# Four-head graph attention: its preparation by pairs of tiles in a fixed TensorE order, with the first scores as columns of the projection

## The chip, the cores and the metric

The kernel runs on one core of one Trainium2 chip. The metric is the time of one execution on the device in microseconds (us), as the median of several runs. A core has TensorE (PE: matmuls and, on rows of their own, the loads of the stationary operand, PEld), VectorE (DVE), ScalarE (ACT), GpSimd (POOL) and SyncE (SP, which issues DMAs here). Each takes its instructions in order from its own queue and waits on semaphores for the others. Matmul results land in PSUM, from where VectorE or ScalarE brings them to SBUF.

## The reference, cut to what matters

The network has four layers on a graph of N = 2708 nodes with 256 features. Each layer is a graph attention and a feed-forward part, and both add to `x`. The change is in the graph attention of the second layer (layer 1 in the code), which has H = 4 heads of D = 64:

```python
x = _layernorm(x)                               # (2708, 256)
h  = (x @ W).reshape(n, H, D)
si = jnp.einsum('nhd,d->nh', h, a1)             # first scores, one per node and head
sj = jnp.einsum('nhd,d->nh', h, a2)             # second scores
e  = leaky_relu(si[:, None, :] + sj[None, :, :], negative_slope=0.2)
e  = where(adj[:, :, None] > 0, e, -9e15)
att = softmax(e, axis=1)
out = einsum('ijh,jhd->ihd', att, h)            # added to x
```

The kernel never forms `e` by itself. With slope 0.2, exp(leaky_relu(si + sj)) is exp(0.2 si) exp(0.2 sj) max(1, exp(0.8 si) exp(0.8 sj)). The factor exp(0.2 si) falls out of the softmax over j. So three tables are wanted: exp(0.8 si) for all i, spread over all 128 partitions (`big_p`, one row of 2708 columns per head, the same on every partition); exp(0.8 sj) as one number per node on its partition (`ratio`); and exp(0.2 sj), which multiplies the projected features (`V`) and makes the denominators (`low`).

## The kernel before

The nodes are cut into NT = 22 tiles of up to 128 (`tiles`, the last has 20), and the columns into six chunks of up to 512 (`cols = chunks(512)`: five of four tiles, and one of 148 columns with two tiles). `X[:, t, :]` holds tile t with nodes on partitions.

Right before, `slice_ffn` ends with 22 tiles of four matmuls each (tile `po`, L477 through the helper's L139), added to `X` by VectorE (L478). The layer-norm statistics (`net.ln_stats()`, L773) follow each `X` tile closely: `bn_stats` and `bn_aggr` on VectorE (L160, L161), then for each four tiles a square root on ScalarE (L163) and a reciprocal on VectorE (L167).

`gat_heads` (L704) then prepares the tables (L756 to L819) and runs the attention (L820 to L882). Before the loop of the preparation it folds `a1` and `a2` into the weight `W` (`fold_scores`, L768 and L769), so that the second scores are four more columns of the projection weight `w`, and the first scores have a weight of their own, `spread`, whose columns 0, 32, 64 and 96 hold the four heads and the rest zeros. Then, for each chunk of columns:

- for each tile of the chunk: VectorE normalizes it into `f` (L780, helper L124); TensorE transposes its two halves into PSUM `tp` (L781, helper L132); ScalarE copies them into the chunk's `ft` (L782); TensorE projects, 260 columns, into `pv` (L784, helper L139); ScalarE takes two exponentials of the four score columns, into `low` (L787) and `ratio` (L788); VectorE multiplies the features into `V` (L789);
- for the chunk: VectorE sums `ft` (L795); TensorE multiplies `spread` with `ft` into `s1p` (L797), so that each head's first scores stand as a row on partition 0, 32, 64 or 96; ScalarE copies it to `s1` (L799); one-row matmuls with ones (L803) spread each head's row over all partitions into `pp`, four banks of PSUM; ScalarE takes the exponential of all four heads into `big_p` (L804).

A PSUM tile named `tp`, `s1p` or `pp` has one buffer, `pv` two. A matmul of these float32 tiles appears as two records, a transpose as one. After the loop come the mean row for nodes without neighbours (L806 to L815) and the transposed flags of such nodes (L817, L818), sent into the mask by `mark_empty`.

The order of the preparation is the Tile framework's: it arranges each engine's queue by the program's order and by its own estimate of when operands are ready. A pool's memory goes to the next pool when its tiles are released; the attention's `e` tiles (L820) take the place of the preparation's `g1one` and `g1work`. In the attention itself TensorE's order is written out (`tc.manual_schedule`, L826): for each of two pairs of heads and each tile j, ScalarE computes max(1, .) less 1 (L700), VectorE adds one and applies the mask (L701), and TensorE accumulates values (L836) and denominators (L847).

Of the kernel before, what the change touches and what calls it, by code (L numbers as in the profile page):

```python
# [48 lines left out]
def tiles_of(start, length):  # L49
    return range(start // P, (start + length + P - 1) // P)  # L50
# [653 lines left out]
def gat_heads(net, keep):  # L704
# [38 lines left out]
    with ExitStack() as ctx:  # L743
        big = ctx.enter_context(tc.tile_pool(name="g1big", bufs=1))
        big_p = big.tile([P, H, N], F32, name="big_p")
        ratio = big.tile([P, NT, H], F32, name="ratio")
        V = big.tile([P, NT, H, DH], F32, name="V")

        low = big.tile([P, NT, H, 2 * Q - 1], F32, name="low")
# [6 lines left out]
        with ExitStack() as c1:  # L756
            one = c1.enter_context(tc.tile_pool(name="g1one", bufs=1))
            work = c1.enter_context(tc.tile_pool(name="g1work", bufs=3))
            psum = c1.enter_context(tc.tile_pool(name="g1p", bufs=1, space=PSUM))
            fsum = one.tile([P, 2], F32, name="fsum")  # L760
            spread = one.tile([P, 2, P], F32, name="spread")

            w = one.tile([P, 2, H * DH + H], F32, name="w")
            nc.gpsimd.dma_start(w[:, :, : H * DH], a["g1_w"].rearrange("(c p) m -> p c m", p=P))
            av = one.tile([P, 2, DH], F32, name="av")
            for n in range(2):
                nc.gpsimd.dma_start(av[:, n, :], a[f"g1_a{n + 1}"].partition_broadcast(P))
            a1 = fold_scores(net, one, w, av[:, 0, :].unsqueeze(1).to_broadcast([P, H, DH]), H, DH, "a1")  # L768
            a2 = fold_scores(net, one, w, av[:, 1, :].unsqueeze(1).to_broadcast([P, H, DH]), H, DH, "a2")  # L769
            nc.vector.tensor_copy(w[:, :, H * DH :], a2)  # L770
            nc.vector.memset(spread, 0.0)
            nc.vector.tensor_copy(spread.rearrange("p c (h k) -> p c h k", h=H)[:, :, :, 0], a1)
            ln = net.ln_stats()  # L773
            parts = one.tile([P, len(cols), 2], F32, name="parts")
            for n, (n0, nw) in enumerate(cols):
                ft = work.tile([P, 2, 512], F32, name="ft")
                for k, t in enumerate(tiles_of(n0, nw)):
                    r = rows(t)
                    f = work.tile([P, D], F32, name="f")
                    net.normed(f, t, ln)  # L780
                    ps = net.transposed(psum, f, r)  # L781
                    nc.scalar.copy(ft[:, :, k * P : k * P + r], ps[:, :, :r])  # L782
                    pv = psum.tile([P, H * DH + H], F32, name="pv", bufs=2)
                    net.matmul_k(pv[:r], ft[:, :, k * P : k * P + r], w)  # L784
                    s2 = pv[:r, H * DH :]
                    lt = low[:r, t, :, Q - 1]
                    nc.scalar.activation(lt, s2, AF.Exp, scale=SLOPE)  # L787
                    nc.scalar.activation(ratio[:r, t, :], s2, AF.Exp, scale=1.0 - SLOPE)  # L788
                    nc.vector.tensor_tensor(  # L789
                        V[:r, t],  # L790
                        pv[:r, : H * DH].rearrange("p (h d) -> p h d", d=DH),
                        lt.unsqueeze(2).to_broadcast([r, H, DH]),
                        ALU.mult,
                    )
                nc.vector.tensor_reduce(parts[:, n, :], ft[:, :, :nw], AX.X, ALU.add)  # L795
                ps = psum.tile([P, 512], F32, name="s1p")
                net.matmul_k(ps[:, :nw], spread, ft[:, :, :nw])  # L797
                s1 = work.tile([P, 512], F32, name="s1")
                nc.scalar.copy(s1[:, :nw], ps[:, :nw])  # L799
                ps = psum.tile([P, H, 512], F32, name="pp")  # L800
                for h in range(H):
                    row = slice(32 * h, 32 * h + 1)
                    nc.tensor.matmul(ps[:, h, :nw], net.ones[row, :], s1[row, :nw], start=True, stop=True)  # L803
                nc.scalar.activation(big_p[:, :, n0 : n0 + nw], ps[:, :, :nw], AF.Exp, scale=1.0 - SLOPE)  # L804

            nc.vector.tensor_reduce(fsum, parts.rearrange("p n c -> p c n"), AX.X, ALU.add)  # L806
            ps = psum.tile([P, H * DH + H], F32, name="pv", bufs=2)
            one_row = slice(SPARE, SPARE + 1)
            for c in range(2):
                nc.tensor.matmul(  # L810
                    ps[one_row, : H * DH], fsum[:, c : c + 1], w[:, c, : H * DH], start=c == 0, stop=c == 1
                )
            nc.vector.tensor_scalar(
                V[one_row, LAST].rearrange("p h d -> p (h d)"), ps[one_row, : H * DH], 1.0 / N, None, ALU.mult
            )  # L815
            ps = psum.tile([NT, P], F32, name="s1p")
            nc.tensor.transpose(ps, net.empty, net.ident)  # L817
            nc.vector.tensor_copy(net.flags, ps)  # L818
            mark_empty(net)  # L819
# [1630 lines left out]
```

## Time and profile before

| | |
|---|---|
| median of 3 runs | 2646.69 us (2646.11 to 2649.6) |
| the profiled execution | 2647.78 us, span 2646.0 us |
| TensorE busy over the span | 92%, mean granted clock 0.962 |
| VectorE, ScalarE, GpSimd busy | 56%, 40%, 12% |
| the preparation, first `tp` transpose to first L700 | 603.26 to 670.29 us |
| the attention that follows | 670 to about 1000 us, PE busy in all of each 20 us from 680 on |
| projections `pv` of the preparation | 84 records of 128x260 and 4 of the last tile, mean 463 ns and 386 ns |
| exponentials to `big_p` (L804) | 5 of 128x2048, 1877 ns each, one of 128x592, 663 ns |
| granted clock, 603.2 to 618.0 us | 0.65 |

The span runs from the first instruction to the last. Times inside the kernel are counted from the span's start. A row of the profile names a line of the code, an engine, an operation, its output and its inputs; a line can be a helper's, so that the projections of several stages share L139 and are told apart by tile. A matmul's record includes its way through the pipeline, so back-to-back matmuls start closer together than their durations.

### The profile page before, as it was taken

Reading aid. Unit: us, or ns where it says so; the run is one execution under the profiler, and the core shown is the slowest. Engines: PE = TensorE matmul, PEld = TensorE weight load, DVE = VectorE, ACT = ScalarE, POOL = GpSimd, SP = SyncE. Lnnn points to the kernel's source line nnn. Section 1 sums busy time; section 2 is a strip of 40 time slices with the busy share of each in tenths; the row PEclk is TensorE's granted clock in tenths of the full one; section 3 lists DMA queues with packets and bytes.
Section 4 is the critical chain, followed back from the end, with each engine's and each line's share of the span. In section 5 each row is a group of like instructions: output and inputs, shape, how many; then the busy total and the mean of one; then the engine's idle time right before and its main releaser. Section 6 shows DMA issues by size and latency. Waiting matters only on the chain. (4 is left out here: it accounts for less than half of the span.)

```text
span 2646.0 us, 32568 instructions
## 1 busy us (share of the span) xinstructions
PE 2446.7 (92%) x11676; PEld 1581.2 (60%) x11676; DVE 1476.4 (56%) x3258; ACT 1060.2 (40%) x1714; POOL 329.2 (12%) x445
## 2 busy tenths in 40 slices
PE   5999999887999998979799989999899999969998
PEld 4666765574333334468578854444357777747887
DVE  7754348544788886333545457787653222264556
ACT  3444443313787772321434323334422222234454
POOL 1000002100000001134130011222231111110002
PEclk9999999978999999989899999999989999989999
DMA  8899520000000002774310010000231111050001
GB/s 289 281 299 320 172 86 31 3 6 1 1 1 1 1 1 82 170 193 144 91 62 1 1 38 9 19 17 17 101 128 50 33 33 33 22 203 7 1 1 43
DMA packets 106875, 197.70 MB, mean 75 GB/s; under 512 B 8846, under 2 KB 63736, under 8 KB 103876
## 3 DMA queue, kind: packets, MB, share of 16 engines
q1 hardware_dynamic: 88010, 146.82, 17.8%
q0 software_dynamic: 14896, 43.89, 5.1%
q10 hardware_dynamic: 3806, 4.85, 0.6%
q8 instruction: 98, 1.61, 0.3%
q14 instruction: 65, 0.53, 0.1%
HBM read 135.82 MB, written 59.71 MB: 74 GB/s over the span
## 5 line engine op out<-in xcount | busy, mean ns | idle before, releaser
L701 DVE SCALAR_TENSOR_TENSOR e<-e,mask 128x768 f32<-128x768 f32 (+3 forms) x352 | 417.0, 1215 | 241.9 <-ACT e L700 239.1
L700 ACT ACTIVATE e<-big_p,minus_one,ratio 128x768 f32<-128x768 f32 (+3 forms) x352 | 418.6, 1226 | 285.2 <-PE acc L1371 196.8
L1371 PE MATMUL acc<-V,e 128*128 128x257 f32 x1848 | 405.3, 382 | 5.7 <-DVE e L701 5.6
L1371 PEld LDWEIGHTS acc<-V,e 128*128 128x128 f32 x1848 | 352.7, 191 | 58.6 <-issue 7.0
L2125 PE MATMUL h<-w,ft 128*128 (+1 forms) x752 | 233.9, 452 | 1.3 <-DVE yl L1955 1.3
L307 PE MATMUL acc<-F,e 128*128 128x257 f32 (+1 forms) x924 | 212.5, 383 | 3.7 <-DVE e L303 3.4
L836 PE MATMUL acc<-e,V 128*64 128x512 f32 (+1 forms) x1056 | 209.1, 548 | 2.2 <-DVE e L701 2.2
L307 PEld LDWEIGHTS acc<-F,e 128*128 128x128 f32 (+1 forms) x924 | 171.6, 189 | 56.6 <-DVE e L303 29.2
L2142 DVE TENSOR_TENSOR hh<-hh,h 128x682 f32<-128x682 f32 x47 | 40.7, 865 | 243.7 <-PE h L2125 243.7
L2125 PEld LDWEIGHTS h<-w,ft 128*128 128x128 f32 x752 | 135.8, 191 | 57.2 <-issue 1.8
L836 PEld LDWEIGHTS acc<-e,V 128*64 128x64 f32 x1056 | 73.7, 138 | 151.3 <-issue 146.1
L1922 ACT ACTIVATE e<-sc 128x1024 f32<-128x1024 f32 (+4 forms) x131 | 107.1, 863 | 139.2 <-PE sc L1913 116.6
L303 DVE TENSOR_TENSOR e<-e,mask 128x512 f32<-128x512 f32 (+2 forms) x132 | 80.5, 621 | 141.3 <-ACT e L296 139.6
L1944 DVE TENSOR_TENSOR sum<-sum,e 128x1024 f32<-128x1024 f32 (+4 forms) x131 | 135.2, 1032 | 40.1 <-ACT e L1922 19.6
L296 ACT ACTIVATE e<-score 128x512 f32<-128x512 f32 (+2 forms) x132 | 69.4, 544 | 170.4 <-PE score L294 145.1
L2157 PE MATMUL po<-w,ht 114*128 (+1 forms) x564 | 131.5, 383 | 0.9 <-DVE ht L2150 0.9
L1913 PE MATMUL sc<-qt,kt 64*128 64x512 f32 (+5 forms) x568 | 123.9, 555 | 1.4 <-ACT sum L1922 0.9
L2157 PEld LDWEIGHTS po<-w,ht 114*128 114x128 f32 x564 | 107.6, 192 | 23.0 <-DVE ht L2150 8.2
L847 PE MATMUL den<-e,low 128*3 128x512 f32 (+1 forms) x1056 | 117.7, 542 | 0.0
L294 PE MATMUL score<-QK 128*128 128x512 f32 (+2 forms) x264 | 112.0, 553 | 3.4 <-ACT e L296 3.0
L1938 PE MATMUL po<-e,V 128*64 128x512 f32 (+5 forms) x524 | 111.2, 543 | 1.7 <-DVE e L1928 1.7
L2151 ACT COPY ht<-pt 114x256 f32<-114x256 f32 x47 | 17.5, 372 | 201.0 <-DVE ht L2150 201.0
(652 smaller groups left out, 3408.4 us busy)
## 6 DMA issues: line engine op xcount, KB each, us to landing
row<-in_adj SPq DMA_DIRECT2D x21, 1354.0 KB
raw<-in_adjT SPq DMA_DIRECT2D x35, 768.0 KB
hs<-zero SPq DMA_DIRECT2D x8, 2838.0 KB
hidden<-hr SPq DMA_DIRECT2D x32, 256.0 KB
wd<-in_f_wd SPq DMA_DIRECT2D x8, 1024.0 KB
kept<-mask SPq DMA_DIRECT2D x21, 338.5 KB
mask<-kept SPq DMA_DIRECT2D x21, 338.5 KB
w<-in_d_w1T SPq DMA_DIRECT2D x8, 682.0 KB
```

The costliest lines, as they stand in the source:

```text
L294: nc.tensor.matmul(ps[:r, :iw], QK[:, 0, span(j)], QK[:, 1, i0 : i0 + iw], start=True, stop=True)
L307: ended = nc.tensor.matmul(acc[k], e[:r, k * P : (k + 1) * P], F[:r, j, :], start=j == 0, stop=j == NT - 1)
L700: nc.scalar.activation(v, big_p[:, i], AF.Relu, bias=net.minus_one, scale=ratio)
L701: return nc.vector.scalar_tensor_tensor(v, v, 1.0, net.mask[:, j, i], ALU.add, ALU.mult)
L836: nc.tensor.matmul(acc[n][half, :iw], V[:, j, h, :], e[n][:, k, :iw], start=j == 0, stop=j == NT - 1)
L847: nc.tensor.matmul(den[g : g + Q, :iw], low[:, j, h, Q - 1 - q : 2 * Q - 1 - q], e[n][:, k, :iw], start=False, stop=j == NT - 1 and q == Q ...
L1371: nc.tensor.matmul(acc[k][:ri], e[:, k * P : k * P + ri], V[:, j, :], start=j == 0, stop=j == NT - 1)
L1913: nc.tensor.matmul(by_pairs(ps[:r, g], m, iw)[:, :, o:], kt[b, span(j)], qt[b, :, o:iw], start=True, stop=True)
L1938: nc.tensor.matmul(by_pairs(outs[n, p][b], m, iw)[:, :, o:], V[:r, j, g, :], by_pairs(e[:r, g], m, iw)[:, :, o:], start=j == 0, stop=j == ...
L1944: nc.vector.tensor_tensor(total, total, by_heads(e[:r], m, iw)[:, :, :, o:], ALU.add)
L2125: last = nc.tensor.matmul(halves[s, n][:, q, :HALF], fts[s][:, c, :], weights.w13[n][:, es[s], c, q * HALF : (q + 1) * HALF], start=c == 0 ...
L2157: last = nc.tensor.matmul(po, ht[:KP, k, :], w2[:KP, es[s], k, :], start=k == 0, stop=k == KC - 1)
```

## The change

Only the preparation in `gat_heads` is edited, and the tables' formats stay except for `ratio`.

- The folded first-score weights become columns H*DH + H to H*DH + 2H of `w`, and the second-score ones are written straight into `w`: the projection has 264 columns, and each tile's `pv` holds both scores with nodes on partitions. `s1p` and the old `spread` go.
- One exponential with scale 0.8 takes all eight score columns into `ratio`, which is now `[P, NT, 2 * H]`. GpSimd copies its four first-score columns into every 32nd column of one of four `spread` tiles, and TensorE transposes that into PSUM `line`: rows 0, 32, 64 and 96 then hold exp(0.8 si).
- VectorE copies the `line` of a chunk to `s1`; the one-row matmuls spread it over the partitions for two heads at a time (`pp` with two banks); ScalarE copies (no exponential) to `big_p`.
- Transposes go by pairs of tiles (11 pairs): four into one `tp` of two buffers, and one copy of up to 512 elements. TensorE's order is written out: the projection of a pair, the transposes of the pair two ahead, half a chunk of `pp`, the `spread` transposes of the pair before.
- The statistics of tiles 0 to 19 take the root on ScalarE as before; those of tiles 20 and 21 take three Newton steps on VectorE (`Stats.newton`, L169). An exponential of one column, queued behind the last root, loads ScalarE's table.
- `f` has four buffers, `ft` two, `pv` three.

The diff:

```diff
@@ -743,7 +743,7 @@
     with ExitStack() as ctx:
         big = ctx.enter_context(tc.tile_pool(name="g1big", bufs=1))
         big_p = big.tile([P, H, N], F32, name="big_p")
-        ratio = big.tile([P, NT, H], F32, name="ratio")
+        ratio = big.tile([P, NT, 2 * H], F32, name="ratio")
         V = big.tile([P, NT, H, DH], F32, name="V")
 
         low = big.tile([P, NT, H, 2 * Q - 1], F32, name="low")
@@ -758,53 +758,114 @@
             work = c1.enter_context(tc.tile_pool(name="g1work", bufs=3))
             psum = c1.enter_context(tc.tile_pool(name="g1p", bufs=1, space=PSUM))
             fsum = one.tile([P, 2], F32, name="fsum")
-            spread = one.tile([P, 2, P], F32, name="spread")
-
-            w = one.tile([P, 2, H * DH + H], F32, name="w")
-            nc.gpsimd.dma_start(w[:, :, : H * DH], a["g1_w"].rearrange("(c p) m -> p c m", p=P))
+            HD = H * DH
+            w = one.tile([P, 2, HD + 2 * H], F32, name="w")
+            nc.gpsimd.dma_start(w[:, :, :HD], a["g1_w"].rearrange("(c p) m -> p c m", p=P))
             av = one.tile([P, 2, DH], F32, name="av")
             for n in range(2):
                 nc.gpsimd.dma_start(av[:, n, :], a[f"g1_a{n + 1}"].partition_broadcast(P))
-            a1 = fold_scores(net, one, w, av[:, 0, :].unsqueeze(1).to_broadcast([P, H, DH]), H, DH, "a1")
-            a2 = fold_scores(net, one, w, av[:, 1, :].unsqueeze(1).to_broadcast([P, H, DH]), H, DH, "a2")
-            nc.vector.tensor_copy(w[:, :, H * DH :], a2)
-            nc.vector.memset(spread, 0.0)
-            nc.vector.tensor_copy(spread.rearrange("p c (h k) -> p c h k", h=H)[:, :, :, 0], a1)
-            ln = net.ln_stats()
+            for n in range(2):
+                fold_scores(
+                    net, one, w, av[:, n, :].unsqueeze(1).to_broadcast([P, H, DH]), H, DH, f"a{n + 1}",
+                    w[:, :, HD + (1 - n) * H : HD + (2 - n) * H],
+                )
+            spread = [one.tile([P, H, 32], F32, name=f"spread{k}") for k in range(4)]
+            for t in spread:
+                nc.gpsimd.memset(t, 0.0)
+            ln = Stats(net)
+            for t0 in range(0, NT - 2, 4):
+                ln.sums(t0, t0 + 4)
+                ln.roots(t0, t0 + 4)
+            with tc.issue_after(ln.root.ins):
+                nc.scalar.activation(one.tile([P, 1], F32, name="warm"), net.ln_eps, AF.Exp)
+            ln.sums(NT - 2, NT, root=False)
+            ln.newton(one, NT - 2, NT)
             parts = one.tile([P, len(cols), 2], F32, name="parts")
-            for n, (n0, nw) in enumerate(cols):
-                ft = work.tile([P, 2, 512], F32, name="ft")
-                for k, t in enumerate(tiles_of(n0, nw)):
+            steps = [(n, k) for n, (n0, nw) in enumerate(cols) for k in range(0, len(tiles_of(n0, nw)), 2)]
+            fts, lines = {}, {}
+
+            def pair_of(n, k):
+                return list(enumerate(tiles_of(*cols[n])))[k : k + 2]
+
+            def turn(n, k):
+                if k == 0:
+                    fts[n] = work.tile([P, 2, 512], F32, name="ft", bufs=2)
+                pair = pair_of(n, k)
+                ps = psum.tile([P, 2, 2 * P], F32, name="tp", bufs=2)
+                for m, t in pair:
+                    r, o = rows(t), (m - k) * P
+                    f = work.tile([P, D], F32, name="f", bufs=4)
+                    net.normed(f, t, (ln.mean, ln.rstd))
+                    for c in range(2):
+                        nc.tensor.transpose(ps[:, c, o : o + r], f[:r, c * P : (c + 1) * P], net.ident[:r, :r])
+                pw = (len(pair) - 1) * P + rows(pair[-1][1])
+                nc.scalar.copy(fts[n][:, :, k * P : k * P + pw], ps[:, :, :pw])
+
+            def project(n, k):
+                n0, nw = cols[n]
+                for m, t in pair_of(n, k):
                     r = rows(t)
-                    f = work.tile([P, D], F32, name="f")
-                    net.normed(f, t, ln)
-                    ps = net.transposed(psum, f, r)
-                    nc.scalar.copy(ft[:, :, k * P : k * P + r], ps[:, :, :r])
-                    pv = psum.tile([P, H * DH + H], F32, name="pv", bufs=2)
-                    net.matmul_k(pv[:r], ft[:, :, k * P : k * P + r], w)
-                    s2 = pv[:r, H * DH :]
+                    pv = psum.tile([P, HD + 2 * H], F32, name="pv", bufs=3)
+                    net.matmul_k(pv[:r], fts[n][:, :, m * P : m * P + r], w)
                     lt = low[:r, t, :, Q - 1]
-                    nc.scalar.activation(lt, s2, AF.Exp, scale=SLOPE)
-                    nc.scalar.activation(ratio[:r, t, :], s2, AF.Exp, scale=1.0 - SLOPE)
+                    nc.scalar.activation(ratio[:r, t, :], pv[:r, HD:], AF.Exp, scale=1.0 - SLOPE)
+                    nc.scalar.activation(lt, pv[:r, HD : HD + H], AF.Exp, scale=SLOPE)
+                    nc.gpsimd.tensor_copy(spread[t % 4][:r, :, 0], ratio[:r, t, H:])
                     nc.vector.tensor_tensor(
                         V[:r, t],
-                        pv[:r, : H * DH].rearrange("p (h d) -> p h d", d=DH),
+                        pv[:r, :HD].rearrange("p (h d) -> p h d", d=DH),
                         lt.unsqueeze(2).to_broadcast([r, H, DH]),
                         ALU.mult,
                     )
-                nc.vector.tensor_reduce(parts[:, n, :], ft[:, :, :nw], AX.X, ALU.add)
-                ps = psum.tile([P, 512], F32, name="s1p")
-                net.matmul_k(ps[:, :nw], spread, ft[:, :, :nw])
-                s1 = work.tile([P, 512], F32, name="s1")
-                nc.scalar.copy(s1[:, :nw], ps[:, :nw])
-                ps = psum.tile([P, H, 512], F32, name="pp")
-                for h in range(H):
-                    row = slice(32 * h, 32 * h + 1)
-                    nc.tensor.matmul(ps[:, h, :nw], net.ones[row, :], s1[row, :nw], start=True, stop=True)
-                nc.scalar.activation(big_p[:, :, n0 : n0 + nw], ps[:, :, :nw], AF.Exp, scale=1.0 - SLOPE)
+                if m * P + P >= nw:
+                    nc.vector.tensor_reduce(parts[:, n, :], fts[n][:, :, :nw], AX.X, ALU.add)
+
+            def line(n, k):
+                if k == 0:
+                    lines[n] = psum.tile([P, 512], F32, name="line")
+                for m, t in pair_of(n, k):
+                    r = rows(t)
+                    nc.tensor.transpose(
+                        lines[n][:, m * P : m * P + r],
+                        spread[t % 4][:r].rearrange("p h k -> p (h k)"),
+                        net.ident[:r, :r],
+                    )
+
+            def broadcast(n):
+                n0, nw = cols[n]
+                s1 = work.tile([P, 512], F32, name="s1", bufs=2)
+                nc.vector.tensor_copy(s1[:, :nw], lines.pop(n)[:, :nw])
+                for h0 in range(0, H, 2):
+                    yield
+                    ps = psum.tile([P, 2, 512], F32, name="pp")
+                    for m in range(2):
+                        row = slice(32 * (h0 + m), 32 * (h0 + m) + 1)
+                        nc.tensor.matmul(ps[:, m, :nw], net.ones[row, :], s1[row, :nw], start=True, stop=True)
+                    nc.scalar.copy(big_p[:, h0 : h0 + 2, n0 : n0 + nw], ps[:, :, :nw])
+
+            with tc.manual_schedule(engines={mybir.EngineType.PE}):
+                for s in range(2):
+                    turn(*steps[s])
+                later = iter(())
+                for s in range(len(steps) + 1):
+                    if s < len(steps):
+                        project(*steps[s])
+                    if s + 2 < len(steps):
+                        turn(*steps[s + 2])
+                    next(later, None)
+                    if s:
+                        line(*steps[s - 1])
+                        n, k = steps[s - 1]
+                        if s == len(steps) or steps[s][0] > n:
+                            for _ in later:
+                                pass
+                            later = broadcast(n)
+                            next(later)
+                for _ in later:
+                    pass
 
             nc.vector.tensor_reduce(fsum, parts.rearrange("p n c -> p c n"), AX.X, ALU.add)
-            ps = psum.tile([P, H * DH + H], F32, name="pv", bufs=2)
+            ps = psum.tile([P, HD + 2 * H], F32, name="pv", bufs=3)
             one_row = slice(SPARE, SPARE + 1)
             for c in range(2):
                 nc.tensor.matmul(
@@ -813,7 +874,7 @@
             nc.vector.tensor_scalar(
                 V[one_row, LAST].rearrange("p h d -> p (h d)"), ps[one_row, : H * DH], 1.0 / N, None, ALU.mult
             )
-            ps = psum.tile([NT, P], F32, name="s1p")
+            ps = psum.tile([P, 512], F32, name="line")[:NT, :P]
             nc.tensor.transpose(ps, net.empty, net.ident)
             nc.vector.tensor_copy(net.flags, ps)
             mark_empty(net)
```

## The prediction

> **What bounds the kernel now.** I read the page first. TensorE is busy 92% of the span, but that mean hides the stage that is edited, and the page's chain of waits that ended last covers only the last tiles of the kernel. So I looked up the edited lines and found that they run once, from the first `tp` transpose of this preparation at 603.26 us to the first attention activation (L700) at 670.29 us: 67.0 us of 2646.0. Then I asked for the busy time by stretches (columns: stretch, length, busy time and count of PE, PEld, DVE, ACT, POOL, then clock, DMA share, GB/s).
>
> ```profile
> 562.00:603.00 41.00, 40.25 (x177) 33.72 (x176) 25.80 (x81) 2.13 (x7) 0.17 (x1) 0.95 0.00 0
> 603.20:618.00 14.80, 11.52 (x29) 7.14 (x30) 5.05 (x14) 3.92 (x14) 0.32 (x3) 0.65 0.00 0
> 628.80:639.50 10.70, 8.22 (x39) 4.89 (x36) 4.25 (x9) 4.55 (x14) 0.00 (x0) 1.00 0.00 1
> ```
>
> The stage before (rows from 562) fills TensorE; a steady chunk of four tiles (628.8 to 639.5) fills no engine: PE is marked busy for 8.2 of 10.7 us with pipeline latency counted in, VectorE and ScalarE for under 5. The first chunk takes 14.8 us, most of it at half clock. It is a latency chain, and the waits of 603 to 672 us name it (engine, tile, line, releaser: total, times, longest).
>
> ```profile
> DVE V L789 <- ACT ratio L788: 24.7, 19, 5.0
> ACT low L787 <- PE pv L139: 23.7, 16, 2.2
> DVE f L124 <- PE tp L132: 16.8, 9, 2.5
> PEld pv L139 <- ACT ft L782: 16.6, 17, 2.0
> PE pv L139 <- ACT ft L782: 12.2, 17, 1.7
> ACT s L799 <- PE s1p L139: 9.0, 6, 2.5
> ```
>
> Each engine waits for the next: TensorE transposes, ScalarE copies, TensorE projects, and the next tile's transposes stand behind that projection. The timeline of one steady tile shows the ring (start, duration, engine, line).
>
> ```profile
> 634.42 0.37 ACT L782 COPY ft<-tp 128x256 f32<-128x256 f32 x1
> 634.85 1.14 PE L139 MATMUL pv<-w,ft 128*128 128x260 f32 x4 [0.46 <-ACT ft L782]
> 635.83 0.38 PE L132 MATMUL tp<-ident,f 128*128 128x128 f32 x2
> 636.25 0.37 ACT L782 COPY ft<-tp 128x256 f32<-128x256 f32 x1
> 636.67 0.74 PEld L139 LDWEIGHTS pv<-w,ft 128*128 128x128 f32 x4 [0.70 <-ACT ft L782]
> ```
>
> From copy to copy is 1.83 us. PE streams for about 1.1 us of it and waits for the copy the rest. A chunk adds `s1p`, its copy, `pp`: 10.72 us between the same transposes of two chunks. Last, the attention after 670: PE is busy 20.00 of every 20 us from 680 to 1000, and DMA moves about 1 GB/s, so what the preparation saves should arrive at the end whole.
>
> **What the Trainium skill says.** "ScalarE: Activation LUTs", section "What ACT_TABLE_LOAD costs", prices a change of table set at 1283 ns plus a drain; here the load at 605.48 took 1.28 us, and TensorE stood 1.71 us before the next projection (607.33). "TensorE: Matmul & The Clock Gate", Part 1, says that the array falls to half clock after a window of about 3.4 us with too little work and returns after a busy one; the trace agrees, with half-clock stretches of 10.2 us (607.0 to 617.2), 3.4 us (from 654.8) and 6.8 us (from 671.9). Part 3 there says that matmuls on different 32-row strips run at once; the trace agrees: the four heads' `pp` matmuls start 7 ns apart, and two passes of four take 1.07 us to the next weight load. So two heads take as long as four.
>
> **The change part by part.**
>
> *Removed from TensorE.* `s1p`, 24 matmuls: 20 of 512 columns 0.43 us apart, so 1.72 us a chunk, about 9 us in all.
>
> *Added to TensorE.* One transpose a tile of `spread`, 22 x 0.107 us (pitch of the `tp` records) = 2.35. Four more columns on 88 projections: pitch 0.219 for 260, under 0.004 each, 0.3 in all. `pp` in two halves: 2 x 1.07 a chunk in place of 1.07, so +5.3 over five chunks and about +0.5 on the last. By work alone TensorE gains only 1 us; the worth is in the order.
>
> *Order.* `turn` of pair s+2 stands behind `project` of pair s, with two `tp` and three `pv` buffers: a copy has a whole step to land, and the ring opens. TensorE then sets the pace if no other engine does. Per step ScalarE has one copy of 512 columns (0.585, row L799), one of 1024 (L804: 0.66 at 592, 1.88 at 2048, so 1.02) and four small exponentials (about 0.07 apart in records of 0.17; 0.5 together): 2.1 us. VectorE has 2 x 0.41 (L124), 2 x 0.425 (L789), half of 1.21 (L795) and half of a 512-column copy out of PSUM (0.69, row L871): 2.6 us. GpSimd has two copies of 128x4 that no row shows; between the 0.10 of a 128x1 memset (L424) and the 0.98 of a 128x256 add (L1971) I take 0.2; even 2 x 0.98 fits. TensorE has two projections (8 x 0.219 + 0.107 for the weight load behind `pp` = 1.86), four transposes (0.43), a half of `pp` (1.07), two `spread` transposes (0.21): 3.57 us. It is the longest.
>
> *Statistics and table.* The last two tiles go to `newton`: 12 small VectorE operations about 0.2 us apart where rows L346 to L348 occur, 2.4 us, against a root and a reciprocal. They stand behind tile 21's sums (ends 604.2), so until about 606.6, and the `f` of tiles 4 and 5 may stand behind them until 607.4, where `turn(2)` wants them at 606.5: 0 to 1.5 us of wait, I take 1.0. Four `f` buffers let tiles 0 to 3 be normed early, as three are now (573.2). The Exp table loads behind the fifth root (600.3 to 601.9), while ScalarE idles under the `po` matmuls: free; uncovered it would be the 1.7 us it is now. The folding drops two copies and one memset hidden under `po`; four GpSimd memsets (0.47 for 128x440, so below that each) are needed only at 606: free. `ratio` with eight columns: same record within 0.01 us.
>
> *Sum, from 603.26.* First transposes 0.43, latency and wait 0.33 (603.67 to 603.83 plus the modelled end), copy 0.585, 0.05: projection starts after 1.4. Eleven projections 11 x 1.86 = 20.5; nine turns 3.9; ten `spread` pairs 2.1; eight halves of `pp` before the last step 8.6: 35.0 (the small last pair rounded off). Newton 1.0. Half clock for one window somewhere in the opening, 0 to 3.4, I take 1.0. The tail: chunk 4's line must be copied by VectorE (0.33 + 0.69 + 0.05), then `pp` and its copy alternate on one buffer: 1.40 + 1.02 + 1.45 + 1.02, and for 148 columns twice (0.84 + 0.42): 8.5. The mean row's four matmuls (L810, 1.02 now) can stand behind the last `pp`, and their operand `w` lies where the first `e` goes; with a slow clock in this sparse tail, 1.2 (0 to 3). Together 1.4 + 35.0 + 1.0 + 1.0 + 8.5 + 1.2 = 48.1 us against 67.0: 18.9 saved. The attention restarts at half clock in both, as now from 671.9.
>
> The profiled execution took 2647.78 (span 2646.0 and 1.78 around it), 1.09 above the median 2646.69. 2647.78 - 18.9 = 2628.9, on the median's footing 2627.8.
>
> **Rivals.**
>
> *In-order queues cost a part.* ScalarE's and VectorE's order is still the planner's; a 1.02 us copy or the 1.21 us reduce put ahead of the copy that TensorE wants next stalls it. For: a copy stands next to the small activations now, and `V` waits 24.7 us for `ratio`. Against: every hand-over has about a step of 3.5 us of slack. One such miss of 1.0 us in each of nine steps: 9 us gone, 2637.
>
> *Slower: the clock.* Place: the eleven steps. If transposes and one-row matmuls count for little to the gate, the stage may run at half clock: 35 us of TensorE work would take 70, so 83 us in place of 67.0 and 2663. "TensorE: Matmul & The Clock Gate", Part 4, says that a transpose does not count as busy in the same way; no run here shows it alone. It decides when more than 18.9 + 1.0 us of full-speed work falls under half clock (1.0 is in the sum already), and is slower by over 0.2% from 25. Against: the steady chunks now hold full clock with 0.88 + 0.21 us of streaming in 1.82; a step will have 1.75 of plain projection in 3.57 and no idle time.
>
> *Nothing arrives.* The planner's memory release or the first attention tile waits for something that stays at 670, or the order is much as before. For: `mark_empty` is sent at 670.48. Against: it feeds only the last tile's mask, and no DMA runs here. 2646.7.
>
> *Better.* The attention's first activation needs only the first 1536 columns of `big_p`; if it goes ahead of the last copies the tail hides 3 to 4 us, and without the two allowances: about 25 saved, 2621 or less.
>
> **How the numbers follow.** As forecast, saving 13 to 25 (2621.5 to 2634): 0.64. Queue stalls (2634 to 2641): 0.17. Better: 0.06. No change: 0.06. Half clock, slower: 0.07. 0.2% of this time, 5.3 us, is about what a measurement tells from no change; the first three are faster (0.87), then 0.06 and 0.07. Range 2620 to 2640: it takes in the allowances' ends and most of the stalls and leaves out the last two cases.
>
> **What would show it.** Right: L700's first activation (by its operands) near 651.4 us; steady steps 3.5 to 3.7 us apart between transposes of pairs; clock 1.0 from about 607; the table load near 600.6 under `po`; ten 128x1024 copies to `big_p` of 1.02 us. A step of over 4.3 us with waits of PE on ScalarE shows the first rival; clock 0.5 over most of the stage, the second; an unmoved first activation, the third. Wrong above all if a row of two heads in `pp` costs more than 1.07, or TensorE's fixed order waits on GpSimd.

## The result and the profile after

The changed kernel takes 2629.61 us (median of 4 runs, 2624.74 to 2631.44), the kernel before 2648.07 us beside it (4 runs, 2646.11 to 2649.6): a ratio of 0.9927, with a 95% interval of 0.9915 to 0.9939. The forecast was 2627.8 us. The profiled execution took 2629.6 us, its span is 2627.7 us, and the mean granted clock is 0.962 as before.

| us | before | after | difference |
|---|---|---|---|
| start to first `tp` transpose | 603.26 | 605.59 | +2.3 |
| first `tp` to first L700: the stage | 67.03 | 44.91 | -22.1 |
| first L700 to the end | 1975.7 | 1977.2 | +1.5 |
| first `tp` to first accumulation `acc` | 70.5 | 48.4 | -22.1 |

So the stage gave more than the 18.9 us of the forecast, and some of it is not in the total. Busy times by stretches of the changed kernel (stretch, length, busy time and count of PE, PEld, DVE, ACT, POOL, then clock, DMA share, GB/s):

```profile
562.00:605.50 43.50, 42.59 (x187) 34.81 (x184) 26.64 (x82) 5.22 (x14) 0.76 (x4) 0.93 0.03 5
605.60:618.00 12.40, 12.04 (x67) 9.65 (x68) 11.67 (x40) 5.67 (x23) 2.27 (x11) 1.00 0.01 2
628.50:639.50 11.00, 11.00 (x56) 7.19 (x55) 5.77 (x11) 6.07 (x18) 1.14 (x6) 1.00 0.01 1
605.60:650.50 44.90, 42.17 (x207) 26.90 (x207) 26.94 (x71) 22.37 (x67) 5.96 (x27) 0.96 0.00 1
```

In the steady stretch (628.5 to 639.5) PE is busy for all of 11.00 us, where it was 8.22 of 10.7. The opening, which had clock 0.65, has 1.00. VectorE is busy for 11.67 of the first 12.40 us, and yet TensorE isn't late there. The half clock that is left, 3.8 us, is at the end of the stage, from 646.7. The waits of 603 to 660 us (engine, tile, line, releaser: total, times, longest) now stand on the engines that follow TensorE:

```profile
ACT ratio L811 <- PE pv L139: 11.0, 22, 0.8
DVE V L814 <- ACT low L812: 9.1, 16, 1.9
ACT big_p L844 <- PE pp L843: 9.0, 12, 1.4
ACT ft L802 <- PE tp L800: 3.6, 10, 1.9
PE pv L139 <- ACT ft L802: 0.4, 1, 0.4
```

Before, `pv` waited for `ft` 17 times on PE (12.2 us); it now waits once, at the opening. One whole step, in the timeline of PE and PEld (start, duration, engine, line):

```profile
617.76 1.64 PEld L139 LDWEIGHTS pv<-w,ft 128*128 128x128 f32 x8
619.65 0.60 PE L800 MATMUL tp<-ident,f 128*128 128x128 f32 x4
620.18 1.13 PE L843 MATMUL pp<-s,ones 1*128 1x512 f32 x4
621.24 0.44 PE L828 MATMUL line<-ident,spread 128*128 128x128 f32 x2
621.40 1.64 PEld L139 LDWEIGHTS pv<-w,ft 128*128 128x128 f32 x8
```

From one step's weight loads to the next is 3.64 us (forecast 3.57), with no release wait on any of these rows. The opening and the tail, in the timeline:

```profile
602.97 1.28 ACT L780 ACT_TABLE_LOAD   x1
607.02 2.05 PE L139 MATMUL pv<-w,ft 128*128 128x264 f32 x8 [0.36 <-ACT ft L802]
...
642.49 1.02 PE L871 MATMUL pv<-w,fsum 128*1 128x256 f32 x4
...
650.20 0.41 ACT L844 COPY big_p<-pp 128x296 f32<-128x296 f32 x1 [0.96 <-PE pp L843]
650.50 1.67 ACT L700 ACTIVATE e<-big_p,minus_one,ratio 128x1536 f32<-128x1536 f32 x1
```

The table load lies under the `po` matmuls, which end at 605.0. The projection starts 1.43 us after the first transpose. The mean row (L871) runs in a gap of the tail, at 642.49, long before the last `pp` (649.29). L700 starts right behind the last copy to `big_p`.

### The profile page after: what moved, and what is told of

Its sections match the earlier page's. It is cut to its first block, busy times and chain, and to the rows that moved or that the text cites. A ratio compares the mean times of both kernels' runs of the same rounds, so it can differ in the third digit from the quotient of the medians.

```text
span 2627.7 us, 32580 instructions
## 1 busy us (share of the span) xinstructions
PE 2440.1 (93%) x11674; PEld 1583.9 (60%) x11674; DVE 1479.9 (56%) x3272; ACT 1057.7 (40%) x1703; POOL 335.0 (13%) x471
## 5 line engine op out<-in xcount | busy, mean ns | idle before, releaser
L700 ACT ACTIVATE e<-big_p,minus_one,ratio 128x768 f32<-128x768 f32 (+3 forms) x352 | 418.6, 1226 | 280.5 <-PE acc L1432 193.1
L2218 PE MATMUL po<-w,ht 114*128 (+1 forms) x564 | 129.8, 380 | 0.9 <-DVE ht L2211 0.9
```

The costliest lines, as they stand in the source:

```text
L700: nc.scalar.activation(v, big_p[:, i], AF.Relu, bias=net.minus_one, scale=ratio)
L2218: last = nc.tensor.matmul(po, ht[:KP, k, :], w2[:KP, es[s], k, :], start=k == 0, stop=k == KC - 1)
```

## The experiments

Two theories share the forecast's mechanism but split the saving differently. *Order*: the turns two ahead open the ring, TensorE sets the pace, and each part is worth its TensorE time. *Opening*: much of the saving is the first chunk, with its table load and its half clock. The rivals of the forecast (stalls of in-order queues, half clock, an earlier L700) are tried along with them. All kernels were profiled and compared with the kernel before on the same chip. "Stage" is from the first `tp` to the first L700 in the profiled execution; half clock is the time in us with a granted clock of 0.5 (the other value in these profiles is 1.0), before, in and after the stage.

| kernel | median us | ratio, 95% interval | stage | half clock |
|---|---|---|---|---|
| before | 2648.07 | | 67.03 | 54.6 / 13.7 / 133.1 |
| after | 2629.61 | 0.9927 (0.9915 to 0.9939) | 44.91 | 61.4 / 3.8 / 132.7 |
| after_again | 2630.45 | 0.9926 (0.9910 to 0.9943) | 44.91 | 58.0 / 3.4 / 139.9 |
| before_stats | 2648.98 | 0.9994 (0.9985 to 1.0003) | 67.16 | 64.9 / 17.1 / 133.1 |
| after_old_stats | 2629.24 | 0.9921 (0.9904 to 0.9938) | 45.29 | 64.9 / 3.4 / 140.0 |
| no_ahead | 2644.42 | 0.9980 (0.9971 to 0.9989) | 64.29 | 58.0 / 22.8 / 134.2 |
| order_only | 2635.65 | 0.9948 (0.9931 to 0.9965) | 51.62 | 54.6 / 3.3 / 129.8 |
| tail_on_vector | 2629.34 | 0.9922 (0.9906 to 0.9939) | 45.15 | 58.0 / 3.7 / 119.4 |
| pp_four | 2626.47 | 0.9908 (0.9892 to 0.9925) | 39.25 | 61.4 / 1.0 / 135.5 |
| pp_four_vector | 2628.59 | 0.9913 (0.9896 to 0.9931) | 39.60 | 64.9 / 1.1 / 143.4 |
| after_footing | 2629.71 | 0.9919 (0.9906 to 0.9933) | 44.90 | 61.4 / 3.3 / 137.8 |
| pp_four_again | 2625.44 | 0.9907 (0.9891 to 0.9922) | 39.44 | 54.6 / 1.4 / 142.0 |
| own_line | 2620.68 | 0.9892 (0.9877 to 0.9907) | 36.38 | 58.0 / 0.0 / 129.7 |
| pp_twice (one run) | 2641.18 | | 58.16 | 58.0 / 13.2 / 130.2 |

### after_again: the change once more, beside the first parts

The changed kernel without an edit, as the footing of the next three.

> The changed kernel unmodified, as the footing of the other runs. Theory (fixed order opens the ring): the preparation, from the first transpose to the first attention activation, takes 44.9 us again within 1 us, as its queues are the same; the whole is 15 to 22 us below the kernel before. If the 22 us that the stage gained were partly chance (phase of the clock's windows), the stage would come out 3 us or more away from 44.9. What lies before and after the stage (605.6 and 1977.2 us in the changed kernel, 603.3 and 1975.7 before) should scatter by some us between executions if the 4 us lost there are the clock's windows, and should stay 2.3 and 1.5 above the kernel before if the change causes them.

The stage is 44.91 us, as in the first profile. Before it lie 605.4 us and behind it 1978.1 (605.6 and 1977.2 there). The medians save 19.2 us (2649.65 over 23 runs of the kernel before, to 2630.45).

### before_stats: statistics and table load alone, in the kernel before

```diff
-            ln = net.ln_stats()
+            ln = Stats(net)
+            for t0 in range(0, NT - 2, 4):
+                ln.sums(t0, t0 + 4)
+                ln.roots(t0, t0 + 4)
+            with tc.issue_after(ln.root.ins):
+                nc.scalar.activation(one.tile([P, 1], F32, name="warm"), net.ln_eps, AF.Exp)
+            ln.sums(NT - 2, NT, root=False)
+            ln.newton(one, NT - 2, NT)
+            ln = ln.mean, ln.rstd
```

> The kernel before with only the statistics' part of the change: the last two tiles by Newton steps, and the Exp table loaded behind the fifth root. Order theory: only the opening of the first chunk is mended; stage 63 to 65 us against 67.0, total 2 to 4 us less (0.1%). Rival (the table load and the cold clock that follows it are the greater part): stage 57 us or less, total 10 us less or more. If the VectorE steps delay the first chunk instead, stage 67 to 69.

No gain: 0.9994, the interval includes 1, and the stage is 67.16 us instead of the expected 63 to 65. The first chunk did get shorter, 9.2 us between the first transposes of chunks 0 and 1 (607.47 to 616.63), where the kernel before needs 14.7. But the half clock came later instead (from 642.3). The timeline shows two tiles' projections of this kernel, at full and at half clock (the last bracket is the idle time before them):

```profile
633.55 1.14 PE L139 MATMUL pv<-w,ft 128*128 128x260 f32 x4 [0.46 <-ACT ft L790]
645.43 2.10 PE L139 MATMUL pv<-w,ft 128*128 128x260 f32 x4 [0.46 <-ACT ft L790]
```

The same wait of 0.46 us, and nearly twice the time: the stage had 17.1 us of half clock against 13.7. PE still waits in every tile, and the stage as a whole kept its length.

### after_old_stats: statistics and table load as before, in the changed kernel

The reverse edit: `ln = net.ln_stats()`, and `net.normed(f, t, ln)`, without the `warm` activation.

> The changed kernel with the statistics as before (six roots on ScalarE, the Exp table loaded at the first exponential). Order theory: the load and the wait around it come back once, 1.3 to 3 us, with half clock for one window perhaps 2 more: stage 46 to 50 us. Rival (table load and clock are the greater part): stage 55 us or more.

The stage is 45.29 us, 0.38 longer than in after_again and less than the 46 to 50 expected. The table load has moved into the opening, to the first exponential:

```profile
610.88 1.28 ACT L804 ACT_TABLE_LOAD   x1 [0.61 <-PE pv L139]
```

ScalarE is held for 1.28 us in the opening, and PE goes on with projections whose operands were copied two steps ahead: one step takes 2.82 us in place of 2.44, and the others are as long as before. With either order, then, this part is worth nearly nothing, and the theory *Opening* falls.

### no_ahead: the changed kernel without the turns two ahead

```diff
-                for s in range(2):
-                    turn(*steps[s])
...
+                        turn(*steps[s])
                         project(*steps[s])
...
-                    if s + 2 < len(steps):
-                        turn(*steps[s + 2])
```

> The changed kernel, but the transposes of a pair stand right ahead of the projection of the same pair on TensorE, not two pairs ahead. Order theory: TensorE waits at each of eleven pairs for the end of the transposes, the semaphore and the 0.585 us copy, 0.97 us each, so about 10 us more: stage 54 to 57 us with steps of 4.6 us, and more if the clock falls. Rival (the pairs and the smaller work alone bring the gain, look-ahead doesn't matter): stage 45 to 47 us.

The stage is 64.29 us, more than the 54 to 57 expected at full clock: of the 22.1 us, 19.4 are gone. The busy times by stretches, with the columns as above (clock third from the end):

```profile
605.30:617.00 11.70, 8.88 (x46) 6.98 (x47) 8.66 (x32) 3.82 (x16) 1.38 (x9) 1.00 0.01 1
617.00:640.00 23.00, 19.94 (x73) 11.57 (x72) 10.28 (x22) 8.06 (x24) 1.52 (x8) 0.78 0.00 0
640.00:669.60 29.60, 24.99 (x91) 12.86 (x91) 9.34 (x19) 10.05 (x28) 2.55 (x10) 0.79 0.00 1
```

And two projections of the timeline, a step apart at full clock, with the wait in each:

```profile
616.61 2.05 PE L139 MATMUL pv<-w,ft 128*128 128x264 f32 x8 [0.68 <-ACT ft L802]
621.31 2.05 PE L139 MATMUL pv<-w,ft 128*128 128x264 f32 x8 [0.79 <-ACT ft L802]
```

A step with `pp` is 4.70 us here, 1.06 over the changed kernel's 3.64; the three before it, without `pp`, gain 0.84 to 0.94. Over the ten intervals between the eleven projections that is about 10 us, an estimate from the first five, which run at full clock. The other 9 us go with the half clock: 22.8 us of the stage against 3.8, and half of the difference is 9.5. So the same matmuls with a wait of 0.6 to 0.8 us in each step ran at half clock for a third of the stage.

### order_only: the order with the old scores

260 columns, a folded `spread` of `[P, 2, P]`, and the exponential on `big_p`; `ft` has three buffers. The order, the pairs and the statistics are the change's.

```diff
-                for m, t in pair_of(n, k):
-                    r = rows(t)
-                    nc.tensor.transpose(
-                        lines[n][:, m * P : m * P + r],
-                        spread[t % 4][:r].rearrange("p h k -> p (h k)"),
-                        net.ident[:r, :r],
-                    )
+                n0, nw = cols[n]
+                if k + 2 >= len(tiles_of(n0, nw)):
+                    net.matmul_k(lines[n][:, :nw], spread, fts[n][:, :, :nw])
...
-                    nc.scalar.copy(big_p[:, h0 : h0 + 2, n0 : n0 + nw], ps[:, :, :nw])
+                    nc.scalar.activation(big_p[:, h0 : h0 + 2, n0 : n0 + nw], ps[:, :, :nw], AF.Exp, scale=1.0 - SLOPE)
```

> The changed kernel's pairs, order and statistics, but the computation of before: 260 columns, the first scores of a chunk as one product of 512 columns (1.72 us) in place of the four transposes of exponentials (0.43 us), exponentials where the copies to the 128 partitions are. Order theory: the stage is TensorE's work plus the same head and tail, so 44.9 + 5 x 1.29 + about 0.3 = 51 to 52 us, total 12 to 17 us below the kernel before. Rival (moving the exponentials to the nodes' partitions is what matters): stage 60 us or more. Other rival (the product was hidden too): 45 to 46.

The stage is 51.62 us. So the order (with the statistics) brings 15.4 of the 22.1 us, and the score columns with exponentials on node partitions the other 6.7. A chunk in PE's timeline:

```profile
617.33 2.02 PE L139 MATMUL pv<-w,ft 128*128 128x260 f32 x8
620.78 1.98 PE L139 MATMUL line<-ft,spread 128*128 128x512 f32 x4
625.94 2.02 PE L139 MATMUL pv<-w,ft 128*128 128x260 f32 x8
```

It takes 8.61 us (from 617.33 to 625.94), 1.33 over two steps of 3.64. TensorE's arithmetic gives 1.29: 4 x 0.43 for the product with `spread` less 4 x 0.107 for four transposes. TensorE's time is paid one for one, as it should be where TensorE sets the pace.

### tail_on_vector: another queue for the last copies

```diff
-                    nc.scalar.copy(big_p[:, h0 : h0 + 2, n0 : n0 + nw], ps[:, :, :nw])
+                    copy = nc.vector.tensor_copy if n >= 4 else nc.scalar.copy
+                    copy(big_p[:, h0 : h0 + 2, n0 : n0 + nw], ps[:, :, :nw])
```

> The changed kernel, with the copies of the last two chunks into the tables on VectorE, so that ScalarE's queue has the first attention activation right behind the copy of chunk 3. If only ScalarE's own queue held that activation, it starts 3 to 6 us earlier, at 39 to 42 us from the stage's first transpose, and the first accumulation of values on TensorE comes 2 to 4 us earlier (48.4 us from the first transpose now). If the memory of its output is released only at the last copy, it starts at 44.9 or a little later, as VectorE's copies are longer.

The stage is 45.15 us, no shorter, though nothing is left ahead of L700 on ScalarE. The timeline says what it waits for:

```profile
649.72 5.73 ACT L700 ACTIVATE e<-big_p,minus_one,ratio 128x1536 f32<-128x1536 f32 x4 [7.49 <-PE pp L843]
```

It needs the first 1536 columns of `big_p`, which are long there; it sits idle for 7.49 us, until the last `pp` matmul. That matmul reads the last `s1`, which the program keeps in the memory that the first `e` takes over; whether this is the reason, own_line tries below.

### pp_four and pp_four_again: four heads at once

```diff
-                    yield
-                    ps = psum.tile([P, 2, 512], F32, name="pp")
-                    for m in range(2):
-                        row = slice(32 * (h0 + m), 32 * (h0 + m) + 1)
-                        nc.tensor.matmul(ps[:, m, :nw], net.ones[row, :], s1[row, :nw], start=True, stop=True)
-                    nc.scalar.copy(big_p[:, h0 : h0 + 2, n0 : n0 + nw], ps[:, :, :nw])
+                yield
+                ps = psum.tile([P, H, 512], F32, name="pp")
+                for h in range(H):
+                    row = slice(32 * h, 32 * h + 1)
+                    nc.tensor.matmul(ps[:, h, :nw], net.ones[row, :], s1[row, :nw], start=True, stop=True)
+                for h0 in range(0, H, 2):
+                    nc.scalar.copy(big_p[:, h0 : h0 + 2, n0 : n0 + nw], ps[:, h0 : h0 + 2, :nw])
```

The two banks come from one `tp` buffer and one `pv` buffer.

> The changed kernel with the spread of all four heads over the partitions in one go of four banks, once a chunk, one transpose buffer in place of two and two projection buffers in place of three. If TensorE's work sets the pace and two heads cost as much as four (1.07 us): 4 x 1.07 less in the steps, about 3 less in the tail, stage 37 to 39 us. If the buffers are what lets TensorE run ahead: waits at each step, stage 42 us or more. If two heads cost half of four: stage 43 to 45.

> Four heads in one go, once more, beside the changed kernel on the same chip: stage 39.2 us, first accumulation at 42.8, total 3 to 8 us below the changed kernel. If the clock's windows take it back, as they scatter by some us, the two totals differ by less than 2 us.

The stages are 39.25 and 39.44 us, and the first `acc` comes 42.8 and 43.0 us after the first `tp`, in place of 48.4. Three chunks in PE's timeline:

```profile
618.15 1.14 PE L842 MATMUL pp<-s,ones 1*128 1x512 f32 x8
624.37 1.14 PE L842 MATMUL pp<-s,ones 1*128 1x512 f32 x8
630.58 1.14 PE L842 MATMUL pp<-s,ones 1*128 1x512 f32 x8
```

Eight records take the time that four took (1.14 us), and a chunk is 6.21 us in place of 7.28: 1.07 less, exactly one `pp`. The buffers that were given up cost nothing in the steps; in the opening the second turn waits 0.80 us for the copy of the first, and the projection starts 1.92 us after the first `tp`, not 1.43. On the same chip as after_footing the median of pp_four_again is 4.3 us lower, of the 5.5 us that the stage lost; the intervals of the two ratios still overlap.

### pp_four_vector and own_line: four heads, and what holds the first activation

Both send the last two chunks' copies to VectorE as in tail_on_vector. The second also gives the last chunk's row memory outside the pools that are released:

```diff
+        own = big.tile([P, cols[-1][1]], F32, name="own")
...
-                s1 = work.tile([P, 512], F32, name="s1", bufs=2)
+                s1 = own if n == 5 else work.tile([P, 512], F32, name="s1", bufs=2)
```

> Four heads in one go and the copies of the last two chunks on VectorE. If both act and add: first attention activation 33 to 36 us from the first transpose, first accumulation of values 43 to 46 us from it (48.4 in the changed kernel), total 3 to 8 us below the changed kernel. If VectorE's queue is then what is late, as its copies stand ahead of the first mask operation, the accumulation gains less than 2 us more than with four heads alone.

> Four heads in one go, the copies of the last two chunks on VectorE, and the last chunk's row in memory of its own that no attention tile takes over. If the release of that row's memory is what held the first attention activation when the copies were already on VectorE, it starts at 36 to 37 us from the first transpose (39.6 then) and the first accumulation at 41 to 42 us. If something else held it, nothing moves: 39 to 40 and 43.

Without memory of its own the stage is 39.60 us, not 33 to 36, and the median is no lower than pp_four's on the same chip (2628.59 and 2626.47 us). L700 waits again for the last reader of `s1`:

```profile
647.05 5.74 ACT L700 ACTIVATE e<-big_p,minus_one,ratio 128x1536 f32<-128x1536 f32 x4 [5.93 <-PE pp L842]
```

With it, L700 starts 36.4 us after the first `tp`, as expected, and ahead of the last `pp`:

```profile
640.39 10.11 ACT L700 ACTIVATE e<-big_p,minus_one,ratio 128x1536 f32<-128x1536 f32 x7 [2.70 <-PE line L829]
642.62 0.88 PE L843 MATMUL pp<-own,ones 1*128 1x148 f32 x8 [2.27 <-DVE own L838]
645.32 2.04 PE L918 MATMUL den<-big_p,zero 1*128 1x512 f32 x2 [1.50 <-ACT e L700]
```

The theory of the memory release is right about L700. But the attention gained nothing by it: the first `acc` comes at 647.29, 43.3 us after the first `tp` as in pp_four, and not at 41 to 42. PE runs the last `pp` and the opening of the denominators `den` first. That `pp` waited for VectorE's copy into `own` (642.27), which stood behind two copies into `big_p` in VectorE's queue (640.00 to 642.35): the queue that was to help had become the late one. `den` starts at 645.32; the profile names an L700 that ends at 645.18, but VectorE's last work on the stage's PSUM ends at 645.17, so which of the two held it is not shown. It then takes 2.04 us at half clock, as in the change (2.07; 1.09 at full clock in the kernel before). This kernel is the fastest of all, 2620.68 us (2620.36 to 2622.25) against 2629.71 for the change on the same chip, and their runs don't overlap. Yet its last 4.8 us over pp_four_again do not come ahead of the first `acc`: in these two profiles the part behind the first `acc` is 6.2 us shorter, with 12.3 us less half clock behind L700. Why that came in all four runs stays open.

### after_footing and pp_twice: the footing of the last runs, and twice the one-row products

The changed kernel again:

> The changed kernel again, beside the next two on one chip: stage 44.9 us, first accumulation of values 48.4 us from the first transpose, total 15 to 22 us below the kernel before.

Its stage is 44.90 us; the medians save 19.55 us (2649.26 over 9 runs to 2629.71).

```diff
-                    for m in range(2):
+                    for m in (0, 1, 0, 1):
```

> The changed kernel with each one-row product for the 128 partitions issued twice, 1.07 us more TensorE work per step. If TensorE sets the pace: steps of 4.71 in place of 3.64 us, stage 44.9 + 8 x 1.07 + 3 to 4 in the tail = 56 to 58 us. If the other engines do: stage under 50 us. If such one-row products count for little to the clock's gate, half clock appears in the steps and the stage is over 60.

PE's timeline of a step:

```profile
622.01 1.95 PE L139 MATMUL pv<-w,ft 128*128 128x264 f32 x8
626.52 1.95 PE L139 MATMUL pv<-w,ft 128*128 128x264 f32 x8
```

A step is 4.51 us, 0.87 more and not 1.07. The granted clock stays 1.00 through the steps (616 to 640 us), although only 1.78 of 4.51 us is projection (eight records 0.222 apart), and the rest transposes and one-row products. The half clock of this stage, 13.2 us, lies in the tail, from 649.3. The stage is 58.16 us (expected 56 to 58).

## Why the prediction was right, and where its sizes were off

**The ring.** The forecast said that each engine waits for the next and that turns two ahead open this ring. Shown: with the turns put back behind their projections 19.4 of 22.1 us return (no_ahead), and PE waits for `ft` in every step (8.1 us in 11 waits), as it did before in most tiles (12.2 us in 17).

**The pace.** It said that TensorE sets the pace with 3.57 us a step; 3.64 was measured in the five full steps with `pp`. Three runs change TensorE's work and find it in the stage: +1.33 a chunk (order_only), -1.07 (pp_four), +0.87 a step (pp_twice). Two heads cost as much as four, as forecast (`pp` rows of 1.13 and 1.14 us). Where the forecast sums TensorE's work before and after to a gain of 1 us, its terms give about 0.5; nothing rests on it.

**The sum of the stage.** It was 48.1 us and came to 44.9. The worked terms held: the head 1.43 for 1.4, the eleven steps 35.4 for 35.0 (607.02 to 642.40, where the slot of the tenth pair's `line` transposes ends), the tail 8.1 for 8.5 (to 650.50). What was mis-sized are the three allowances, 3.2 us together, which were not needed. Newton's steps (1.0): the `f` of tiles 4 and 5 were computed at 606.05 and 606.47, ahead of the Newton operations (from 606.76), and the transposes that want them come at 608.90 without a wait. Half clock in the opening (1.0): the clock is 1.00 from 605.6. The mean row behind the last `pp` with a slow clock (1.2): the row ran in a gap at 642.49. The slow clock did come, from 646.7; each row of the last two `pp` takes 0.86 us, where the kernel before has 0.53 at full clock, and the tail with it is still below its sum.

**Statistics and table.** The forecast counted the covered table load as free and the uncovered one as 1.7 us. In the changed kernel the uncovered one costs 0.38 (after_old_stats). Alone in the kernel before, the part brings nothing that can be measured (before_stats). The load itself takes 1.28 us in each; what it costs the kernel was decided by the slack behind it.

**The total.** The forecast passed the stage's saving to the end whole, 18.9 us. The stage saved 22.1, the profiled pair 18.2. The missing 3.8 us are 2.3 before the stage, where the code differs only in the statistics, the folding and the memsets, and 1.5 behind it, where it is the same. The first is the clock: over all fourteen profiles the stage starts anywhere from 603.3 to 608.2, but with half of the half-clock time before it taken off, at 574.9 to 576.9. This kernel's start has 6.8 us more half clock (61.4 against 54.6), which is worth 3.4 us. The Trainium skill, "TensorE: Matmul & The Clock Gate", Part 1, "What's actually happening", says that the gate's window is free-running; the unlike starts of one and the same code agree with that (pp_four and pp_four_again: 606.4 and 603.9 us, with 61.4 and 54.6 of half clock). The 1.5 us are not explained by this: with half of the half-clock time taken off, the rest is 1909.2 before and 1910.8 after, and lies between 1907.9 and 1913.3 over all profiles. So the forecast's total is as near as it is because two errors offset each other: allowances that weren't needed, and a part of the saving that was lost elsewhere. That is luck.

The medians of after_again and after_footing save 19.2 and 19.6, so a part of the 22.1 is missing there too. One profile a kernel can't tell whether the change causes this, but every run has its mean granted clock: 0.9621 on average over the 13 runs of the changed kernel, 0.9619 over 39 of the kernel before. Had only the stage lost its 10 us of half clock, the mean would be 0.0016 higher (an estimate from 13.7 and 3.8 us), nearly four times the standard error of the difference. So about as much half clock came back outside the stage, and not in one execution alone. Where, and by what, is open.

**The rivals.** *In-order queues*: no stall, every full step with `pp` took 3.64 to 3.65 us; the 1.02 us copies (1.01 measured) and GpSimd's small copies (0.19 to 0.36 for an assumed 0.2) fit in the slack. *Half clock*: not in the steps of the change, not even with the one-row products doubled; it came where PE waits, in each tile or step (before, before_stats, no_ahead) or in the tail. That rival named another cause, the kind of matmul, and at the shares tried here it did not show; the waits did. Part 4 of the same page of the Trainium skill says that a transpose doesn't count as busy in the same way; a step with 0.64 us of transposes in 3.64 held the full clock here, and no run has transposes alone. *Better*: L700 stood behind the last copies (and the memory of its output would have held it as well: tail_on_vector, own_line), so it did not occur. Where it was brought about (own_line) the first accumulation was not earlier, so the 3 to 4 us of that rival were not to be had in this way. *Nothing arrives* was wrong: L700 moved from 670.3 to 650.5.

## What to carry to other kernels

In a ring of transposing, copying and multiplying, issue the transposes far enough ahead that no engine waits for the one before it, and then count the engine that sets the pace: its microseconds came back one for one here, those of the others did not. A wait of under a microsecond in each step costs more than its sum, because the clock can fall with it; and a wait removed alone can come back as half clock. Look at what the next stage's first instruction really waits for, memory that is released included, and at what its follower waits for, before moving work between queues.

## What the runs showed of the hardware that was not expected

- Repeating a pair of one-row products on the same row strips costs 0.87 us, where the pair alone takes 1.07 (pp_twice): the weight loads of the repeat (at 624.86 and 625.29 in the step that starts at 622.01) run under matmuls.
- A table load of 1.28 us ahead of the first exponentials, inside the stage, cost it 0.38 us (after_old_stats).
- A stage with as much work and 5.5 us less in its first chunk took as long as before (67.16 against 67.03 us), with 17.1 in place of 13.7 us of half clock (before_stats).
- Half clock came, from 626.2 us, in a stage where no single wait of PE had been longer than 0.80 us (no_ahead).
- Nearly the same instructions before the stage took up to 5 us more or less between executions (603.3 to 608.2), with 54.6 to 64.9 us of half clock; identical ones, in two profiles of one kernel, 2.4 us (pp_four and pp_four_again).
